# Two-layer GNN kernel: message biases added by a rank-one product on TensorE, evicted by ScalarE, and 72 constant fills moved to the head of GpSimd's queue

## The chip, the cores and the metric

The kernel runs on one core of one Trainium2 chip. The metric is the device time of one execution in microseconds (us). A profile is one further execution, taken by the hardware profiler; it has a time of its own.

## The reference

There are 12,500 nodes with 128 features and 412,500 directed edges sorted by destination. Only the first layer matters here:

```python
h = relu(layernorm(x))
Xs = h[src]
m_data = Xs @ W_data.T + b_data
m_ctrl = Xs @ W_control.T + b_control
msg = where(edge_types == 0, m_data, m_ctrl)
agg = segment_sum(msg, dst)
x = x + relu(agg + (h @ W_self.T + b_self))
```

The second layer gates each message with a tanh of two projections and sums it again by destination.

## The kernel before

**The stages.** The trace shows a front of some 357 us, then loop 0 (layer 0's aggregation, to about 3,390 us), the change to layer 1, and loop 1 (layer 1's aggregation, to the end). The change lies wholly in the front and in what loop 0 does first.

**The front** interleaves two pieces of work, both written as Python generators: `nodes()`, with 14 batches of 7 blocks of 128 nodes, and the search (`edges`, `windows`, `places`/`sought`). For each batch of `nodes()` the program takes four steps of the search; before the fourteenth batch the search is run out. A list scheduler at compile time orders each engine's queue; nothing is reordered at run time, and an engine waits at the head of its queue.

For one block `nodes()` does this: ScalarE makes `h` (L381, layer norm and ReLU); TensorE transposes it into PSUM (`pt`, L384); ScalarE copies that to `hT` (L386); TensorE multiplies by the three weight matrices side by side (`py`, 128 x 384, fp32, L388, two records a product in the profile); VectorE adds the biases while it moves `py` from PSUM to `y` (L390). For one batch VectorE also takes the statistics (L218, L219), GpSimd fills the 129th column of `y` with ones and zeros (L378, L379), SP writes the message rows to the DRAM table `table1` (L391), ScalarE's queue issues the write of the self term (L395), and ScalarE and GpSimd split `h` into three bf16 parts (L398 to L402). `pt`, `py`, `hT`, `h`, `xb` and `y` have two buffers each.

```python
y = pool.tile([P, NBATCH, 3, D + 1], F32, name="y")
nc.gpsimd.memset(y[:, :, 0:2, D:], 1.0)
nc.gpsimd.memset(y[:, :, 2, D:], 0.0)
...
py = ps_y.tile([P, 3, D], F32, name="py")
nc.tensor.matmul(py.rearrange("p k d -> p (k d)"), hT,
                 wT.rearrange("p k d -> p (k d)"), start=True, stop=True)
nc.vector.tensor_add(y[:, i, :, :D], py, bias)
```

The search first reads and transposes the edge lists (`edges`: `raw_...` loads on SP's queue, VectorE arithmetic, transposes at L513, copies `col` at L515), then finds the windows of each chunk of edges (L416 to L445), then locates edges by GpSimd's indirect DMAs: 21 steps of counting (`junk`, L540), 21 `line` gathers (L550), and 7 triples of `g` gathers (L588), each followed by a chain of VectorE operations from L600 to L637, transposes (L581) and copies (L582, L641). `g` has one buffer, so a triple starts when the chain before it has let go.

**Loop 0** works on 469 groups of four tiles of 128 edges. For a group GpSimd issues four indirect gathers from `table1` (`M`, L690; eight buffers of four gathers), VectorE makes a one-hot matrix (`oh`, L701) and TensorE sums (`acc`). Between two groups TensorE works on a dense part for the last 42 node blocks: `oq` and `oc` on VectorE (L794, L796), the product `pa`, its eviction `A` on ScalarE (L799), and the product `z` of `A` with `H`. TensorE products are kept in program order; all of them show as L259, the line of a helper.

Between the groups the program also takes one step at a time of `prepared_for()`. Its first step fills DRAM with zeros (14 large transfers on SP's queue, L726). Its second step makes two flags, one for each loop. For each flag GpSimd fills a row `early` piece by piece with constants known when the program is built (8 and 64 fills, L747), and VectorE compares it with the window starts (L748). `early` has one buffer, so the fills for the second flag wait until the first flag's use of it is over (L754).

```python
early = pool.tile([1, n], F32, name="early")
for c in range(n):
    if c == 0 or done[c] != done[c - 1]:
        nc.gpsimd.memset(early[:, c:], float(done[c]))
nc.vector.tensor_tensor(early, BASE[0:1, :n], early, op=ALU.is_lt)
```

`brow` is a row of the two message biases, each followed by a one, that the dense part of loop 0 uses as one row of a product (the rows `misc<-brow,n` of the profile).

Of the kernel before, what the change touches and what calls it, by code (L numbers as in the profile page):

```python
# [9 lines left out]
F32 = mybir.dt.float32  # L10
# [4 lines left out]
ALU = mybir.AluOpType  # L15
# [3 lines left out]
P = 128  # L19
D = 128  # L20
# [16 lines left out]
def kernel(  # L37
# [32 lines left out]
    nc = tc.nc  # L70
# [93 lines left out]
    ones = consts.tile([P, P], F32, name="ones")  # L164
# [4 lines left out]
    BASE = consts.tile([P, NCK], F32, name="BASE")  # L169
# [165 lines left out]
    with ExitStack() as first:  # L335
# [6 lines left out]
        nc.gpsimd.iota(half[:, P:], pattern=[[1, NCOL]], base=1, channel_multiplier=0,  # L342
                       allow_small_or_imprecise_dtypes=True)
        wz = layer0.tile([P, 2, D + 1], F32, name="wz")
        brow = layer0.tile([1, 2, D + 1], F32, name="brow")
        nc.gpsimd.memset(H[:, :, 3 * D:], 1.0)
        nc.gpsimd.memset(wz[:, :, D:], 0.0)
        nc.gpsimd.memset(brow, 1.0)
        nc.vector.tensor_copy(brow[:, :, :D], bias[0:1, 0:2, :])

        pool = first.enter_context(tc.tile_pool(name="loop0", bufs=1))
        OK = pool.tile([P, 2], F32, name="OK")
# [5 lines left out]
        def nodes():  # L358
            with tc.tile_pool(name="nodes", bufs=2) as pool, \
                    tc.tile_pool(name="nodes_t", bufs=2, space=PSUM) as ps_t, \  # L360
                    tc.tile_pool(name="nodes_y", bufs=2, space=PSUM) as ps_y:
                wT = pool.tile([P, 3, D], F32, name="wT", bufs=1)
                shared["tmin"] = pool.tile([P, TD], F32, name="tmin", bufs=1)
                for k, w in enumerate((w_data, w_control, w_self)):
                    wk = pool.tile([P, D], F32, name="wk", bufs=1)
                    nc.scalar.dma_start(wk, w)
                    pt = ps_t.tile([P, D], F32, name="pt")
                    nc.tensor.transpose(pt, wk, ident)
                    nc.scalar.copy(wT[:, k, :], pt)
                nc.vector.tensor_copy(wz[:, :, :D], wT[:, 0:2, :])  # L370

                for b0 in range(0, NB, NBATCH):
                    xb = pool.tile([P, NBATCH, D], F32, name="xb")
                    load_nodes(xb, b0)
                    rs, shift = scales(pool, xb)
                    h = pool.tile([P, NBATCH, D], F32, name="h")
                    y = pool.tile([P, NBATCH, 3, D + 1], F32, name="y")
                    nc.gpsimd.memset(y[:, :, 0:2, D:], 1.0)  # L378
                    nc.gpsimd.memset(y[:, :, 2, D:], 0.0)  # L379
                    for i in range(NBATCH):  # L380
                        nc.scalar.activation(h[:, i, :], xb[:, i, :], AF.Relu,  # L381
                                             bias=shift[:, i:i + 1], scale=rs[:, i:i + 1])
                        pt = ps_t.tile([P, P], F32, name="pt")
                        nc.tensor.transpose(pt, h[:, i, :], ident)  # L384
                        hT = pool.tile([P, P], F32, name="hT")
                        nc.scalar.copy(hT, pt)  # L386
                        py = ps_y.tile([P, 3, D], F32, name="py")
                        nc.tensor.matmul(py.rearrange("p k d -> p (k d)"), hT,  # L388
                                         wT.rearrange("p k d -> p (k d)"), start=True, stop=True)
                        nc.vector.tensor_add(y[:, i, :, :D], py, bias)  # L390
                    nc.sync.dma_start(  # L391
                        table1[b0 * P * 2:(b0 + NBATCH) * P * 2, :].rearrange(
                            "(b p t) d -> p b (t d)", p=P, t=2),
                        y[:, :, 0:2, :].rearrange("p b t d -> p b (t d)"))
                    nc.scalar.dma_start(agg1[b0 * P:(b0 + NBATCH) * P, :].rearrange(  # L395
                        "(b p) d -> p b d", p=P), y[:, :, 2, :])
                    part = H[:, b0:b0 + NBATCH, :]
                    nc.scalar.copy(part[:, :, :D], h)  # L398
                    nc.gpsimd.tensor_sub(h, h, part[:, :, :D])
                    nc.scalar.copy(part[:, :, D:2 * D], h)  # L400
                    nc.gpsimd.tensor_sub(h, h, part[:, :, D:2 * D])
                    nc.scalar.copy(part[:, :, 2 * D:3 * D], h)  # L402
                    yield
# [318 lines left out]
        def prepared_for(pool):  # L722
            none = pool.tile([P, D], F32, name="none")
            nc.vector.memset(none, 0.0)
            for b0 in range(0, NB, NBATCH):
                nc.sync.dma_start(agg3[b0 * P:(b0 + NBATCH) * P, :].rearrange(  # L726
                    "(b p) d -> p b d", p=P), none[:, None, :].to_broadcast([P, NBATCH, D]))
            nc.sync.dma_start(agg3[NB * P:, :], none)
            nc.sync.dma_start(agg1[NB * P:, :D], none)
            nc.sync.dma_start(agg1[NB * P:, D:], none[:, :1])  # L730
            yield

            need = pool.tile([P, NCK], F32, name="need")
            bad = pool.tile([P, 2], F32, name="bad")
            nc.vector.tensor_scalar(bad, OK, -1.0, 1.0, op0=ALU.mult, op1=ALU.add)
            for k, n, visits, rng in ((0, NC0, MORE0, RNG0), (1, NC2, MORE1, RNG1)):
                nc.vector.tensor_copy(need[:, :n], more[:, :n])
                nc.vector.tensor_scalar(need[:, n:], more[:, n:], 1.0, bad[:, k:k + 1], op0=ALU.add,
                                        op1=ALU.mult)
                nc.vector.tensor_copy(visits, need[0:1, :])  # L740
                bounds(pool, need, rng)

                done, upper = settling[k]
                early = pool.tile([1, n], F32, name="early")
                for c in range(n):
                    if c == 0 or done[c] != done[c - 1]:
                        nc.gpsimd.memset(early[:, c:], float(done[c]))  # L747
                nc.vector.tensor_tensor(early, BASE[0:1, :n], early, op=ALU.is_lt)  # L748
                late = pool.tile([1, n], F32, name="late")
                nc.vector.tensor_scalar(late, BASE[0:1, :n], float(upper - P), None,  # L750
                                        op0=ALU.is_gt)
                nc.vector.tensor_add(early, early, late)
                flag = pool.tile([1, 2], F32, name="flag")
                nc.vector.tensor_reduce(flag[:, 0:1], early, AX.X, ALU.max)  # L754
                nc.vector.tensor_reduce(flag[:, 1:2], need[0:1, :], AX.X, ALU.max)
                nc.vector.tensor_reduce(flag[:, 0:1], flag, AX.X, ALU.max)
                nc.vector.tensor_scalar(flag[:, 0:1], flag[:, 0:1], 0.5, None, op0=ALU.is_gt)
                nc.vector.tensor_copy(AGAIN[:, k:k + 1], flag[:, 0:1])
            yield

            keys = flat_d[T1 - TF:T1 - TF + TDX, :].rearrange("(p t) e -> p (t e)", p=NP)
            at_q = src_q.rearrange("(p t) e -> p (t e)", p=NP)
            at_b = src_b.rearrange("(p t) e -> p (t e)", p=NP)
            W = TDX * P // NP // 13
            for w in range(13):
                ws = slice(w * W, (w + 1) * W)
                shape = [NP, W // 16, 16]
                both = pool.tile([NP, W // 16, 3, 16], F32, name="both")
                nc.sync.dma_start(both.rearrange("p a k e -> p (a k e)"),
                                  keys[:, 3 * w * W:3 * (w + 1) * W])  # L770
                key = both[:, :, 1, :]
                col = pool.tile(shape, F32, name="part")
                nc.vector.tensor_scalar(col, key, 1.0 / P, None, op0=ALU.mult)
                col = floored(pool, col, shape, "part")
                q1 = pool.tile(shape, F16, name="q1", bufs=2)
                nc.vector.scalar_tensor_tensor(q1, col, -float(P), key, op0=ALU.mult, op1=ALU.add)
                nc.sync.dma_start(at_q[:, ws], q1.rearrange("p a e -> p (a e)"))
                up = pool.tile(shape, F32, name="part_up")
                nc.vector.tensor_scalar(up, col, float(NB), None, op0=ALU.is_ge)
                b1 = pool.tile(shape, F16, name="b1", bufs=2)  # L780
                nc.vector.scalar_tensor_tensor(b1, up, -float(NB), col, op0=ALU.mult, op1=ALU.add)
                nc.sync.dma_start(at_b[:, ws], b1.rearrange("p a e -> p (a e)"))
                yield
# [624 lines left out]
```

## Time and profile before

| | us |
|---|---|
| median of 4 runs (lowest, highest) | 7045.01 (7003.73, 7071.27) |
| time of the profiled execution | 7036.41 |
| span of its trace, first to last instruction | 7034.6 |
| PE / DVE / ACT / POOL busy over the span | 5611.8 / 4834.7 / 3176.1 / 3946.5 |
| DVE bias adds of the front (L390, 98) | 53.8 |
| PE message products of the front (L388, 98 in 196 records) | 107.0 |
| last `g` gather of the search, start | 340.95 |
| first `acc` product of loop 0, start | 357.57 |

PE is TensorE, PEld its weight loads, DVE VectorE, ACT ScalarE, POOL GpSimd, SP the engine that only issues DMAs. A row of a timeline gives start, duration, engine, line, operation and, in brackets, the idle time just before and what ended it. "issue" is time for which the profile shows no wait, "remote" a wait whose end it cannot put down to an instruction. PEclk is the TensorE clock that was granted, as a share of full speed; it is read by stage, since a product takes as long as the clock in its stage allows.

### The profile page before, as it was taken

How to read it: one execution, taken by the hardware profiler on the slowest of the kernel's cores; microseconds unless marked ns; L12 is line 12 of the kernel's file. 1: busy time of each engine (PE TensorE's matmuls, PEld its weight loads, DVE VectorE, ACT ScalarE, POOL GpSimd, SP SyncE). 2: the span in 40 equal slices, each digit the busy share in tenths (PEclk: the TensorE clock that was granted, in tenths of full speed). 3: DMA queues.
4: the chain of work that ended last, by engine and by line, in shares of the span. 5: the costliest groups of instructions: out<-in, count | busy, mean ns of one | idle time of the engine just before them, and what ended most of it. 6: DMA issues, size and time to landing. Idle time of an engine off the chain costs nothing. (4 is left out here: it accounts for less than half of the span.)

```text
span 7034.6 us, 108029 instructions
## 1 busy us (share of the span) xinstructions
PE 5611.8 (80%) x33125; PEld 4401.1 (63%) x33126; DVE 4834.7 (69%) x16324; ACT 3176.1 (45%) x9121; POOL 3946.5 (56%) x4224
## 2 busy tenths in 40 slices
PE   5458888888888888888488885888888888888886
PEld 2236666666666666666333332787877877788776
DVE  7656666666576666666477775777777777777775
ACT  5334444444444444444222222655555555555553
POOL 2456656655565656656255655555555555555554
PEclk7669999999999999999799997989999988998898
DMA  6432222222221222221455553122222222222221
GB/s 173 137 91 48 55 49 51 57 57 56 48 69 47 66 49 59 60 56 48 112 145 141 146 139 92 46 53 52 52 54 54 53 54 53 52 53 54 51 52 50
DMA packets 488695, 497.97 MB, mean 71 GB/s; under 512 B 156109, under 2 KB 385897, under 8 KB 488109
## 3 DMA queue, kind: packets, MB, share of 16 engines
q0 software_dynamic: 131360, 274.09, 16.1%
q1 hardware_dynamic: 328141, 201.08, 10.1%
q10 hardware_dynamic: 28608, 15.78, 0.9%
q8 instruction: 271, 4.44, 0.3%
q14 instruction: 315, 2.58, 0.1%
HBM read 415.88 MB, written 74.70 MB: 70 GB/s over the span
## 5 line engine op out<-in xcount | busy, mean ns | idle before, releaser
L974 POOL DMA_INDIRECT M<-table,ix x2128 | 2020.4, 949 | 1563.9 <-issue 806.8
L690 POOL DMA_INDIRECT M<-table,ix x1876 | 1795.4, 957 | 1212.1 <-issue 464.2
L799 ACT CAST A<-pa 128x392 bf16<-128x392 f32 x2688 | 1279.1, 486 | 1506.2 <-PE pa L259 679.6
L259 PE MATMUL z<-H,A 128*128 128x385 bf16 x8232 | 1927.4, 336 | 24.1 <-PE pa L259 15.1
L259 PEld LDWEIGHTS <-A 128*128 128x128 bf16 x8232 | 1134.3, 139 | 893.8 <-issue 607.7
L794 DVE TENSOR_SCALAR oq<-piota,QI 128x128 bf16<-128x128 f16 x2688 | 747.9, 278 | 921.4 <-PE z L259 432.2
L259 PE MATMUL acc<-M,oh 128*128 128x128 f32 (+1 forms) x8008 | 1190.4, 295 | 155.1 <-DVE oh L995 72.2
L259 PEld LDWEIGHTS acc<-M,oh 128*128 128x128 f32 x8008 | 1105.9, 206 | 316.8 <-issue 128.1
L259 PE MATMUL pa<-oc,oq 128*128 128x392 bf16 x2688 | 905.0, 337 | 421.3 <-issue 237.0
L796 DVE TENSOR_SCALAR oc<-piota,CI 128x392 bf16<-128x392 f16 x2688 | 1108.5, 412 | 0.0
L259 PE MATMUL z<-A,HS 128*128 128x128 f32 x6664 | 1010.7, 292 | 93.5 <-issue 77.8
L259 PE MATMUL pa<-oc,oe 128*128 128x196 f32 x4352 | 920.6, 354 | 181.1 <-issue 69.1
L259 PEld LDWEIGHTS z<-A,HS 128*128 128x128 f32 x6664 | 942.9, 205 | 111.3 <-issue 86.4
L259 PEld LDWEIGHTS pa<-oc,oe 128*128 128x128 f32 x4352 | 773.0, 205 | 232.6 <-issue 87.9
L1169 ACT COPY A<-pa 128x392 f32<-128x392 f32 x1088 | 498.0, 484 | 924.5 <-PE pa L259 411.0
L987 ACT ACTIVATE gate<-e,M 128x1 f32<-128x1 f32 x2128 | 516.8, 292 | 650.0 <-DVE only L980 253.2
L980 DVE SCALAR_TENSOR_TENSOR only<-piota,dl,pd 128x128 f32<-128x128 f32 x2128 | 736.9, 346 | 49.5 <-remote 19.6
L1159 ACT ACTIVATE oe<-oq,eb 128x128 f32<-128x128 f32 x2176 | 685.1, 393 | 102.0 <-DVE oq L1151 50.3
L995 DVE TENSOR_SCALAR oh<-piota,dl,e 128x128 f32<-128x128 f32 x2128 | 725.4, 403 | 0.1
L1154 DVE TENSOR_TENSOR oc<-piota,cb 128x784 f32<-128x784 f32 x544 | 525.0, 965 | 29.3 <-remote 11.9
L1151 DVE TENSOR_TENSOR oq<-piota,qb 128x512 f32<-128x512 f32 x544 | 370.6, 681 | 41.9 <-ACT oe L1159 41.9
L259 PE MATMUL ev<-ms,which 98*8 98x512 f32 x552 | 302.9, 632 | 90.6 <-DVE ms L1073 79.4
(271 smaller groups left out, 3390.8 us busy)
## 6 DMA issues: line engine op xcount, KB each, us to landing
M<-table,ix POOLq DMA_INDIRECT x4004
qs<-src_q SPq DMA_DIRECT2D x138, 256.0 KB
bs<-src_b SPq DMA_DIRECT2D x138, 256.0 KB
table<-y SPq DMA_DIRECT2D x14, 903.0 KB
xb<-in_x_dram SPq DMA_DIRECT2D x26, 448.0 KB
o<-agg SPq DMA_DIRECT2D x100, 64.0 KB
agg<-y ACTq DMA_DIRECT2D x14, 451.5 KB
ga<-agg SPq DMA_DIRECT2D x14, 451.5 KB
```

The source lines that it names most:

```text
L259: tc.keep_in_program_order(nc.tensor.matmul(*args, **how))
L690: tc.keep_in_program_order(nc.gpsimd.indirect_dma_start(out=M[:, s, :], out_offset=None, in_=table1, in_offset=bass.IndirectOffsetOnAxis(a ...
L794: nc.vector.tensor_scalar(oq, iota_q, QI[:, k:k + 1], None, op0=ALU.is_equal)
L796: nc.vector.tensor_scalar(oc, iota_c, CI[:, k:k + 1], None, op0=ALU.is_equal)
L799: nc.scalar.copy(A[:, i], pa)
L974: tc.keep_in_program_order(nc.gpsimd.indirect_dma_start(out=M[:, s, :], out_offset=None, in_=table2, in_offset=bass.IndirectOffsetOnAxis(a ...
L980: nc.vector.scalar_tensor_tensor(only, iota_1, dl[:, s:s + 1], pd, op0=ALU.is_equal, op1=ALU.mult, accum_out=e[:, s:s + 1])
L987: nc.scalar.activation(gate[:, s:s + 1], e[:, s:s + 1], AF.Tanh, bias=M[:, s, D:])
L995: nc.vector.tensor_scalar(oh[:, s, :], iota_1, dl[:, s:s + 1], e[:, s:s + 1], op0=ALU.is_equal, op1=ALU.mult)
L1154: nc.vector.tensor_tensor(oc, iota_c[:, None, :].to_broadcast([P, 4, NC1]), cb[:, us, None].to_broadcast([P, 4, NC1]), op=ALU.is_equal)
L1159: nc.scalar.activation(oe[:, k, :], oq[:, k, :], AF.Copy, scale=eb[:, 4 * u + k:4 * u + k + 1])
L1169: nc.scalar.copy(A[:, 4 * u + k:4 * u + k + 2, :], pa)
```

## The change

The biases become a second product into the same PSUM tile: a row of ones (one partition, 128 columns) times a row that holds all three biases and the constants of the 129th column. `py` and the weight tile are widened to 129 columns for each of the three parts, with zeros in the weights' last column; `brow` gets a third part. ScalarE then copies `py` to `y` whole, in place of VectorE's add, and GpSimd's two fills for each batch are gone. Separately, the 72 fills of the flags' rows are issued where the front's constants are made, into two tiles of their own (`taken`) that stay allocated, in place of between groups 1 and 2 of loop 0.

```diff
-        brow = layer0.tile([1, 2, D + 1], F32, name="brow")
+        brow = layer0.tile([1, 3, D + 1], F32, name="brow")
-        nc.gpsimd.memset(brow, 1.0)
-        nc.vector.tensor_copy(brow[:, :, :D], bias[0:1, 0:2, :])
+        nc.gpsimd.memset(brow[:, 0:2], 1.0)
+        nc.gpsimd.memset(brow[:, 2], 0.0)
+        nc.vector.tensor_copy(brow[:, :, :D], bias[0:1, :, :])
+        taken = []
+        for k, (done, _) in enumerate(settling):
+            t = layer0.tile([1, len(done)], F32, name="taken%d" % k)
+            for c in range(len(done)):
+                if c == 0 or done[c] != done[c - 1]:
+                    nc.gpsimd.memset(t[:, c:], float(done[c]))
+            taken.append(t)
...
-                wT = pool.tile([P, 3, D], F32, name="wT", bufs=1)
+                wT = pool.tile([P, 3, D + 1], F32, name="wT", bufs=1)
+                nc.gpsimd.memset(wT[:, :, D:], 0.0)
-                    nc.scalar.copy(wT[:, k, :], pt)
-                nc.vector.tensor_copy(wz[:, :, :D], wT[:, 0:2, :])
+                    nc.scalar.copy(wT[:, k, :D], pt)
+                nc.vector.tensor_copy(wz[:, :, :D], wT[:, 0:2, :D])
...
-                    nc.gpsimd.memset(y[:, :, 0:2, D:], 1.0)
-                    nc.gpsimd.memset(y[:, :, 2, D:], 0.0)
...
-                        py = ps_y.tile([P, 3, D], F32, name="py")
+                        py = ps_y.tile([P, 3, D + 1], F32, name="py")
                         nc.tensor.matmul(py.rearrange("p k d -> p (k d)"), hT,
-                                         wT.rearrange("p k d -> p (k d)"), start=True, stop=True)
-                        nc.vector.tensor_add(y[:, i, :, :D], py, bias)
+                                         wT.rearrange("p k d -> p (k d)"), start=True, stop=False)
+                        nc.tensor.matmul(py.rearrange("p k d -> p (k d)"), ones[0:1, :],
+                                         brow.rearrange("p k d -> p (k d)"), start=False,
+                                         stop=True)
+                        nc.scalar.copy(y[:, i], py)
...
-                done, upper = settling[k]
+                upper = settling[k][1]
                 early = pool.tile([1, n], F32, name="early")
-                for c in range(n):
-                    if c == 0 or done[c] != done[c - 1]:
-                        nc.gpsimd.memset(early[:, c:], float(done[c]))
-                nc.vector.tensor_tensor(early, BASE[0:1, :n], early, op=ALU.is_lt)
+                nc.vector.tensor_tensor(early, BASE[0:1, :n], taken[k], op=ALU.is_lt)
```

## The prediction

> **What bounds the kernel now.** I read the granted clock by stage first, then the stretches of the front, the waits of each engine, the costliest groups, and last the timelines of POOL and PE where loop 0 begins.
>
> Busy time in four stretches of the front (edge reading; windows and counting; line gathers; `g` triples). Columns: stretch, length, busy us of PE, PEld, DVE, ACT, POOL, granted TensorE clock, DMA share, GB/s.
>
> ```profile
> 24.00:120.00 96.00, 59.47 (x210) 34.75 (x209) 70.06 (x215) 58.68 (x137) 22.23 (x32) 0.76 0.74 216
> 120.00:180.00 60.00, 28.93 (x94) 15.01 (x93) 59.16 (x122) 27.00 (x62) 11.52 (x13) 0.73 0.32 85
> 180.00:246.00 66.00, 35.54 (x82) 16.95 (x81) 33.49 (x157) 26.63 (x69) 35.73 (x36) 0.76 0.59 168
> 246.00:310.00 64.00, 32.09 (x90) 15.31 (x89) 49.83 (x118) 26.16 (x62) 25.84 (x25) 0.66 0.43 121
> ```
>
> The reader sees that no one engine bounds the front. DVE does from 120 to 180 us (59.2 of 60). In 24 to 120 DVE, DMA, PE and ACT all lie between 61% and 74%. From 180 us on the search is a chain of gathers and VectorE work, and no engine is over 78%. In loop 0 (460 to 3380 us) PE is busy 2504 of 2920 us at a clock of 0.96, so the loop runs at PE's pace, 6.3 us for a group, while POOL's four gathers of 1.25 us need 5.0. A delay of loop 0's start is therefore not won back: it goes through to the end.
>
> Waits that the change touches, in the front and at loop 0's start: total, times, longest.
>
> ```profile
> DVE y L390 <- PE py L388: 21.3, 26, 2.1
> ...
> POOL y L378 <- DMA agg<-y: 39.8, 8, 10.1
> ...
> POOL early L747 <- DVE flag L754: 19.7, 1, 19.7
> ...
> POOL early L747 <- DMA ci_d<-C: 16.8, 1, 16.8
> ```
>
> DVE stands still for 21.3 us because an add is at the head of its queue before its product is there; the search's VectorE work stands behind it. The last two waits hold POOL at the flags' fills. What they hold back shows in POOL's timeline (start, duration):
>
> ```profile
> 340.95 0.95 POOL L588 DMA_INDIRECT g<-flat_d,rows  x1 [0.30 <-issue]
> 358.72 1.36 POOL L747 MEMSET early<- 1x67 f32 x8 [16.83 <-DMA ci_d<-C]
> 379.79 11.82 POOL L747 MEMSET early<- 1x76 f32 x64 [19.71 <-DVE flag L754]
> 391.77 0.95 POOL L690 DMA_INDIRECT M<-table,ix  x1 [0.16 <-issue]
> ...
> 440.56 0.94 POOL L690 DMA_INDIRECT M<-table,ix  x1 [0.30 <-issue]
> 453.07 0.95 POOL L690 DMA_INDIRECT M<-table,ix  x1 [11.57 <-PE pa L259]
> ```
>
> From 341.9 to 391.8 us POOL issues no gather, though six of the eight `M` buffers are empty. Then it issues 40 in a row. PE over the same time:
>
> ```profile
> 395.09 0.77 PE L259 MATMUL acc<-M,oh 128*128 128x129 f32 x2 [14.61 <-DMA M<-table,ix]
> ...
> 439.35 0.48 PE L259 MATMUL pa<-oc,oq 128*128 128x392 bf16 x1 [27.95 <-issue]
> ...
> 447.04 0.49 PE L259 MATMUL pa<-oc,oq 128*128 128x392 bf16 x1 [6.25 <-ACT A L799]
> ```
>
> PE starves 14.6 us for the third group. Then comes something odd: with all data there, PE, DVE and ACT nearly stop (4.7, 28.0 and 6.3 us idle on PE) until POOL's row of gathers is over. The start of layer 1 shows the same: 28 gathers without a pause from 3481 to 3517 us, and after some 14 of them VectorE stands:
>
> ```profile
> 3481.22 0.94 POOL L974 DMA_INDIRECT M<-table,ix  x1 [98.31 <-issue]
> ...
> 3514.22 0.75 DVE L1073 SCALAR_TENSOR_TENSOR ms<-bs,pidx,gp 98x512 f32<-98x512 f16 x1 [10.92 <-issue]
> ```
>
> I call this the freeze: about 13 gathers (16 us) into an unbroken row the other engines stop, until some 5 us after its end. Two cases make it likely, not sure.
>
> **The change part by part.** Rows for the prices (busy us, mean ns):
>
> ```profile
> L388 PE MATMUL py<-wT,hT 128*128 128x384 f32 x196 | 107.0, 664 | 44.8 <-ACT hT L386 22.9 <-DVE y L390 19.5 <-DVE mv L219 1.0
> L390 DVE TENSOR_TENSOR y<-py,bias 128x384 f32<-128x384 f32 x98 | 53.8, 552 | 22.1 <-PE py L388 21.3
> ...
> L799 ACT CAST A<-pa 128x392 bf16<-128x392 f32 x2688 | 1279.1, 486 | 1506.2 <-PE pa L259 679.6
> ...
> L259 PE MATMUL misc<-wz,zT 128*64 128x129 f32 x336 | 57.6, 296 | 0.5 <-ACT n L815 0.5
> L259 PE MATMUL misc<-brow,n 1*64 1x129 f32 x336 | 57.2, 290 | 0.0
> ```
>
> *The flags' fills.* They cost 1.4 + 11.8 = 13.2 us of POOL wherever they stand. At the head of its queue POOL is idle for 29.3 us (from 3.5 to 32.7 us), so they cost nothing there; behind them stands the new fill of `wT`'s last column, ready near 17 us, and `wT` is first used at 25.1. If that cover were gone, up to 13.2 us would be lost once. They are moved past 40 gathers of `M`, and no DMA moves with them. Without them the 24 gathers of groups 2 to 7 can follow the last `g` gather at 342 us. PE's first `z` comes at 378.7 us; group 2 follows at about 381, and two more groups at 6.3 us put group 4 at 393.6 in place of 451.1: 57.5 us at the most. The freeze eats some of it. It now falls into the row of 24 gathers, 342 to 372 us: it would begin near 358 and end near 377, 19 to 21 us in which the building of `A` stands. The ends are 19 (as in layer 1) and the whole 38.9 + 14.6 of today. I take 21, by the number of gathers: 57.5 - 21 = **36 us gained**, between 4 and 57.
>
> *DVE.* 98 adds go (53.8 us), and 21.3 us of waits with them. This counts only where the search's VectorE work sets the pace. By stretch the adds are 16.9, 10.1, 15.2 and 11.6 us, the waits 10.6, 2.2, 3.3 and 6.6. In 120 to 180 all 12.3 count; in 246 to 310 the chain of a triple takes 14 to 17 us with node work around it and 11.0 without (326.95 to 337.99), so I count half of 18.2, 9; in 180 to 246 DVE waits 28.9 us for gathers, so a quarter of 18.5, 5; in 24 to 120 half of 27.5, 14. Sum: 40 us. All of it at most: 75; nothing at least.
>
> *PE.* 98 products of 387 columns are new. A product with one row costs what one with 128 rows costs (290 against 296 ns), so each is as dear as L388's pair, 1.09 us: 107 us, between 79 (0.81 us a pair, as near 126 us at full clock) and 162 (1.65, at half clock). PE's busy time in 24 to 310 is 156 us of 286; 263 still fits, but bunches no longer do: the search's transposes (L513, L416, L581) stand behind twice the products. The three columns more cost under 1%.
>
> [...]
>
> *ACT.* 98 copies of 128x387 from PSUM: by L799's row 486 ns, 47.6 us on 138 us busy of 286; the idle 148 hides them. The new wait is the dear part: the copy waits for the product, now two, at the head of ACT's queue. Behind it stand the next `hT` (PE waits for it), `h`, and the search's copies `srcf`, `col`, `QI`, `CI`, `yw`; for `col` wait SP's writes. DVE's 21.3 us of waits move here, and each can grow by the second product. The loss by PE and ACT together is shown by no row: nothing if idle time takes it; at most the 107 us of products less PE's waits for DVE's adds (19.5). Nearest is what PE's queue makes the search wait today, 22.9 us for `hT`. I take 22.
>
> *The rest* is nothing: 28 small fills and POOL's 39.8 us wait for `y` go (the add itself never waited for that buffer; if ACT's first copy came early, up to 5.0 us a batch would move to it); `brow`'s copy grows by 128 elements of one partition; SP's `table1` write waits for ACT in place of DVE.
>
> Front: 40 - 22 = **18 us gained**. Sum: 7036.4 - 36 - 18 = 6982.4 us for an execution like the profiled one (span 7034.6, with 1.8 us around it). The median of the runs lies 8.6 us above it, so I forecast **6991 us**. What a measurement of this kernel can tell from no change is about 1%, 70 us.
>
> **The rivals.** Each on the scale of the median.
>
> *All relief, no freeze.* For it: DVE is full from 120 to 180 and PE has 130 us idle. Against: two freezes in the trace. 57 us and the adds and waits of the first, second and fourth stretch (58): 7045 - 115 = 6930.
>
> *The freeze only moves.* Gathers run in a row again, 53.5 us of PE idle return, and the front is neutral: 7045 - 4 = 7041. For it: 38.9 us of the 53.5 have no named cause.
>
> *PE bounds the front (the slower side).* If the clock stays at one half, 98 pairs of products at 1.65 us are 323 us, and PE's other work there is 49: 372 in 286, 86 us over. Less 36: 7045 + 50 = 7095. It decides once PE's mean clock in 24 to 310 is under about 0.65; 0.66 in the last stretch speaks for it, 0.76 in the others against.
>
> *Gathers overtake the search.* Before, eight `M` gathers already went ahead of the last two `g` triples (315 to 326 us). If all 24 do, the search ends 24 x 1.25 = 30 us later: 36 - 30 + 18 = 24 gained, 7021. The fills then are gone, and do not do what they should.
>
> **How the numbers follow.** Forecast 0.40 (own range 6965 to 7020), all relief 0.20, freeze moves 0.18, PE bounds 0.14, overtaking 0.08. For 8 in 10 I reach from the first rival, 6930, to below the slow one, 7085. Faster by over 1% is under 6975: the first rival and a quarter of the forecast, 0.30. Slower by over 1% is over 7115: half of the slow case and a little for a loop order that I can't see, 0.08. Between: 0.62.
>
> **What would show it.** Right: no L747 rows after 340 us, `M` gathers in a row on POOL from about 324, group 4's `acc` near 397 us (451 - 54), the chain of `g` triples ending near 336, DVE under 0.9 in 120 to 180, PEclk in the front over 0.8. Wrong: the last `g` gather later than 345 us, ACT waiting for `py` over 60 us, PE over 90% busy in the front, or a group 4 no earlier than 440.

## The result, and the profile after

The changed kernel is a little **slower**: 7072.11 us median (7027.2 to 7106.04, 52 runs) against 7054.87 us (7003.73 to 7103.06, 78 runs), a ratio of 1.0022 with a 95% interval of 1.0011 to 1.0033; the forecast was 6991 us. Its profiled execution took 7082.81 us, with a span of 7081.1.

The front is where the two traces part. Three marks are used from here on, each read from the timelines: the end of the search (the product `misc<-total,ones`), and the first `acc` of groups 4 and 8 of loop 0.

| us from the span's start | before | after | difference |
|---|---|---|---|
| last `g` gather issued | 340.95 | 394.23 | +53.3 |
| the search ends | 353.5 | 411.9 | +58.4 |
| from there to group 4 | 97.6 | 63.6 | -34.0 |
| group 4 | 451.1 | 475.5 | +24.4 |
| group 468, the last of loop 0 (first `acc`) | 3411.8 | 3440.8 | +29.0 |

Busy time in five stretches of the front, after (columns as for the kernel before: stretch, length, busy us of PE, PEld, DVE, ACT, POOL, granted TensorE clock, DMA share, GB/s):

```profile
24.00:120.00 96.00, 88.36 (x214) 39.85 (x212) 46.33 (x145) 52.40 (x130) 17.03 (x21) 0.75 0.59 176
120.00:180.00 60.00, 54.25 (x140) 23.13 (x140) 43.72 (x120) 35.56 (x82) 7.80 (x6) 0.68 0.37 103
180.00:246.00 66.00, 63.96 (x93) 20.69 (x92) 24.13 (x96) 27.71 (x67) 26.22 (x22) 0.50 0.44 122
246.00:310.00 64.00, 62.13 (x95) 20.68 (x94) 28.43 (x101) 27.42 (x67) 22.02 (x18) 0.50 0.39 106
310.00:358.00 48.00, 46.57 (x88) 17.42 (x89) 23.49 (x56) 23.50 (x57) 14.15 (x12) 0.50 0.41 111
```

PE is now the engine that bounds the front: it is busy 97% of the time from 180 to 358 us. VectorE is relieved, as the change meant it (46.33 us in place of 70.06 in the first stretch). But the clock column reads 0.50 from 180 us on, where it was 0.76 and 0.66. The columns are means over a stretch: each of the 346 entries of the trace's record of the clock holds 1 or 0.5, and it stands at 0.5 from 144.9 to 469.1 us, 324.3 us on end; the last one-row product starts at 392.8. So TensorE has been granted half its speed just where it had the most to do.

The groups that write or read `py` between 24 and 394 us (busy us, mean ns, idle time before them and what ended it):

```profile
L398 PE MATMUL py<-brow,ones 1*128 1x387 f32 x196 | 150.3, 865 | 0.0
L396 PE MATMUL py<-wT,hT 128*128 128x387 f32 x196 | 150.0, 866 | 10.8 <-ACT hT L394 8.8 <-ACT y L401 0.7
L401 ACT COPY y<-py 128x387 f32<-128x387 f32 x98 | 47.3, 482 | 138.9 <-PE py L398 138.7 <-DMA yn_d<-col 0.2
```

The new product costs 150.3 us, and the old one, which was 107.0, has risen to 150.0: 866 ns for each half of it in place of 664. ScalarE's copies cost what was forecast, 482 ns, and wait 138.7 us for the product. The waits between 24 and 394 us show who stands behind (total, times, longest):

```profile
ACT y L401 <- PE py L398: 138.7, 84, 3.2
...
POOL h L410 <- ACT y L401: 56.3, 2, 31.6
...
DVE junk L564 <- DMA line<-flat_d,tile_i: 48.8, 19, 6.8
```

At loop 0's start the fills of `early` are gone from POOL's timeline, and the gathers of `M` begin 8.3 us after the last `g` gather (start, duration, what it is, idle time before it):

```profile
394.23 0.95 POOL L599 DMA_INDIRECT g<-flat_d,rows  x1 [0.30 <-issue]
402.55 1.20 POOL L701 DMA_INDIRECT M<-table,ix  x1 [5.50 <-issue]
...
447.30 0.95 POOL L701 DMA_INDIRECT M<-table,ix  x1 [0.30 <-issue]
```

PE over the same time shows the freeze again, now between groups 0 and 1 (the `acc` of 416.00 and of 448.44): products of `A` come singly, most of them 2.1 to 3.5 us apart, until POOL's row ends.

```profile
416.00 2.06 PE L259 MATMUL acc<-M,oh 128*128 128x129 f32 x8 [3.61 <-DMA M<-table,ix]
...
439.76 0.49 PE L259 MATMUL pa<-oc,oq 128*128 128x392 bf16 x1 [3.01 <-issue]
...
448.44 1.93 PE L259 MATMUL acc<-M,oh 128*128 128x129 f32 x8
```

### The profile page after: what moved, and what is told of

Its sections match the earlier page's. It is cut to its first block, busy times and chain, and to the rows that moved or that the text cites. A ratio compares the mean times of both kernels' runs of the same rounds, so it can differ in the third digit from the quotient of the medians.

```text
span 7081.1 us, 108339 instructions
## 1 busy us (share of the span) xinstructions
PE 5803.2 (82%) x33321; PEld 4456.2 (63%) x33322; DVE 4787.6 (68%) x16226; ACT 3216.1 (45%) x9215; POOL 3941.5 (56%) x4198
## 5 line engine op out<-in xcount | busy, mean ns | idle before, releaser
L259 PEld LDWEIGHTS acc<-M,oh 128*128 128x128 f32 x8008 | 1090.6, 203 | 303.9 <-issue 97.1
L259 PEld LDWEIGHTS pa<-oc,oe 128*128 128x128 f32 x4352 | 792.3, 209 | 223.5 <-ACT oe L1167 96.3
```

Of the source, the lines that this page charges most:

```text
L259: tc.keep_in_program_order(nc.tensor.matmul(*args, **how))
```

## The experiments

Chips differ more than these kernels do: the kernel before took 7128 and 7144 us (medians) on the chips of the first eight runs below and 5904 and 5905 us on those of the last eight, whose loops run faster. Every ratio is against the kernel before on the same chip. The marks of the front come from one trace each and are compared across chips. Where the front is the same, the search's end differs by up to 7.4 us (353.5 in before, 360.9 in before_mb3; 337.6 to 343.8 in the four traces of rows128 with eight or three buffers), so smaller differences are not read. `py` means are for half a product with `wT` and half a product for the biases (bf16rows: the whole of the second).

| kernel | ratio, 95% | clock in 180:246, 246:310 | `py` means, ns | search ends | group 4 |
|---|---|---|---|---|---|
| before | 1 | 0.76, 0.66 | 664 | 353.5 | 451.1 |
| after | 1.0022 (1.0011 to 1.0033) | 0.50, 0.50 | 866, 865 | 411.9 | 475.5 |
| fills_only | 0.9936 (0.9914 to 0.9957) | 0.71, 0.67 | 681 | 383.0 | 421.6 |
| bias_only | 1.0056 (1.0035 to 1.0078) | 0.50, 0.50 | 850, 848 | 407.1 | 505.0 |
| rows128 | 0.9914 (0.9889 to 0.994) | 0.83, 0.84 | 604, 566 | 337.6 | 400.3 |
| bf16rows | 0.9907 (0.9876 to 0.9939) | 0.74, 0.78 | 630, 385 | 353.1 | 395.3 |
| no_product | 0.9925 (0.9901 to 0.995) | 0.74, 0.69 | 650 | 360.7 | 399.2 |
| dve_evicts | 1.0052 (1.0034 to 1.0071) | 0.50, 0.50 | 882, 886 | 426.2 | 495.3 |
| sel128 | 0.9912 (0.9895 to 0.9928) | 0.84, 0.87 | 598, 553 | 341.2 | 406.9 |
| fills_mb3 | 0.9945 (0.9924 to 0.9965) | 0.68, 0.66 | 696 | 365.6 | 406.5 |
| rows32 | 1.0036 (1.0023 to 1.005) | 0.50, 0.50 | 833, 833 | 401.5 | 440.2 |
| rows64 | 1.0025 (1.0016 to 1.0035) | 0.50, 0.50 | 823, 822 | 396.8 | 437.3 |
| paired | 0.9997 (0.9988 to 1.0006) | 0.55, 0.53 | 790, 782 | 381.0 | 421.7 |
| rows128_mb3 | 0.9859 (0.9844 to 0.9874) | 0.82, 0.85 | 608, 570 | 341.2 | 380.3 |
| rows128_same_chip | 0.9931 (0.9918 to 0.9945) | 0.82, 0.86 | 600, 568 | 343.8 | 382.5 |
| rows128_mb3_same_chip | 0.986 (0.9845 to 0.9875) | 0.82, 0.87 | 600, 560 | 341.1 | 381.5 |
| before_mb3 | 0.9923 (0.991 to 0.9937) | 0.71, 0.66 | 680 | 360.9 | 416.5 |
| rows96 | one run: 5868.24 us | 0.81, 0.79 | 628, 586 | 343.9 | 383.0 |

The last column holds the freeze in some rows and not in others. In before and bias_only it stands between groups 3 and 4, in after, rows128, sel128 and dve_evicts between groups 0 and 2. In rows32, rows64, rows96, paired and rows128_same_chip, all on the faster chips with eight buffers, it stands behind group 4 (19 to 26 us from there to group 5), so their group 4 looks early.

### The two parts, one at a time

**fills_only**: the kernel before, with the flags' constants written first and nothing else.

```diff
+        taken = []
+        for k, (done, _) in enumerate(settling):
...
-                nc.vector.tensor_tensor(early, BASE[0:1, :n], early, op=ALU.is_lt)
+                nc.vector.tensor_tensor(early, BASE[0:1, :n], taken[k], op=ALU.is_lt)
```

> The kernel before with the 72 fills moved to the head of GpSimd's queue, and nothing else. Theory (the start of loop 0 gains what was forecast, the front is lost to the products): the search ends where it did, within 10 us of 354, the fourth group's sums start 34 us earlier than before, near 417, and the total is some 34 us under before, near 7020. Rival (the fills' gain seen in the changed kernel only comes from its later start): group 4 near 450, total near 7055.

**bias_only**: the changed kernel, with the constants written where they were.

> The changed kernel with the fills back between the groups of loop 0: only the bias product and ScalarE's eviction are new. Theory: the search ends near 412 us as in the changed kernel, 98 us pass from there to group 4 as before (near 510), and the total is 58 us over before, near 7113; granted clock 0.5 from 145 us to the end of the front. Rival (the two parts are not independent): the total is within 20 us of before.

fills_only took 7095.79 us, by the ratio 46 us (31 to 61) under the kernel before, and 32 by the medians; bias_only took 7170.31, 40 us (25 to 56) over it by the ratio and 42 by the medians. bias_only's marks are those expected: the search ends at 407.1, and 97.9 us later comes group 4. So the change is a gain and a loss that nearly cancel. At group 4 they are 451.1 - 421.6 = 29.5 us gained and 505.0 - 451.1 = 53.9 lost: together +24.4, which is what the changed kernel shows.

The gain did not come in the way expected. In fills_only the gathers of `M` are ready before the search ends, and 25 of them go ahead of the last two `g` triples in POOL's queue, in place of eight. POOL, then VectorE where it takes up these two triples:

```profile
341.25 0.94 POOL L698 DMA_INDIRECT M<-table,ix  x1 [0.30 <-issue]
342.50 0.95 POOL L596 DMA_INDIRECT g<-flat_d,rows  x1 [0.30 <-issue]
...
363.02 0.94 POOL L698 DMA_INDIRECT M<-table,ix  x1 [0.30 <-issue]
364.27 0.95 POOL L596 DMA_INDIRECT g<-flat_d,rows  x1 [0.31 <-issue]
```

```profile
348.25 0.56 DVE L608 TENSOR_TENSOR g<-g,V 128x384 f32<-128x384 f32 x1 [11.28 <-DMA g<-flat_d,rows]
...
369.81 0.56 DVE L608 TENSOR_TENSOR g<-g,V 128x384 f32<-128x384 f32 x1 [12.32 <-DMA g<-flat_d,rows]
```

The same two in the kernel before:

```profile
332.62 0.56 DVE L600 TENSOR_TENSOR g<-g,V 128x384 f32<-128x384 f32 x1 [7.44 <-DMA g<-flat_d,rows]
...
344.06 0.56 DVE L600 TENSOR_TENSOR g<-g,V 128x384 f32<-128x384 f32 x1 [2.39 <-DMA g<-flat_d,rows]
```

PE's transposes for these triples, in fills_only:

```profile
353.12 0.50 PE L589 MATMUL misc<-identh,q 128*128 128x128 f16 x3 [15.60 <-DVE ty L634]
...
374.69 0.50 PE L589 MATMUL misc<-identh,q 128*128 128x128 f16 x3 [16.65 <-DVE col_f L235]
```

PE's two idle times are 11.57 and 6.51 us in the kernel before. The search ends at 383.0 in place of 353.5, 29.5 us later. Of these, 11.8 were there at the fifth triple, whose work on VectorE starts at 327.8 in place of 316.0, before any of these gathers could hold it up; the other 17.7 came behind them. After the search, group 4 follows in 38.6 us in place of 97.6, and no stop stands there. So the rival of the overtaking gathers came true in fills_only. The freeze did not move into the search, but for some 4 us of short waits at its end: VectorE worked on the sixth triple from 348.3 to 357.5 us, as long as before, within POOL's row of gathers. The net came out near the forecast all the same, by luck.

### Is it the one row?

**rows128**: the same product, with 128 rows of 1/128 and the biases in all partitions in place of one row of ones. The same sum, the same number of columns; the constants of the 129th column move into the tile `bias`.

```diff
-                        nc.tensor.matmul(py.rearrange("p k d -> p (k d)"), ones[0:1, :],
-                                         brow.rearrange("p k d -> p (k d)"), start=False,
+                        nc.tensor.matmul(py.rearrange("p k d -> p (k d)"), share[:128, :],
+                                         bias[:128].rearrange("p k d -> p (k d)"), start=False,
```

> The changed kernel with the one-row product replaced by one of 128 rows: ones/128 times the biases held on all 128 partitions, the same 387 columns in fp32 and the same number of products. Theory (a one-row product does not count as activity, so the clock stays at half): the granted clock in the front is 0.85 or more, a product's record falls from 866 to some 450 to 550 ns, the search ends between 340 and 360 us, total 7000 to 7025. Rival (the clock is low for another reason, or the front is simply too full of products): clock 0.5 from 145 us on, records near 866 ns, search end near 412, total near 7072.

**bf16rows**: the biases split in three bf16 parts that together hold the fp32 value, each in 32 partitions (the last 32 hold zeros), so that the product has 128 rows and one record in the profile.

```diff
+                        nc.tensor.matmul(py.rearrange("p k d -> p (k d)"), share,
+                                         bpart.rearrange("p k d -> p (k d)"), start=False,
```

> [...] ScalarE still evicts. Theory (TensorE's time for the bias is the loss, not ScalarE's eviction): the search ends between 330 and 355 us and the total is 6995 to 7020. Rival (ScalarE's eviction and its wait are the loss): the search ends later than 390 us, total near 7060.

**sel128**: rows128 with 127 of the rows of the stationary operand zero.

```diff
-        nc.vector.memset(share, 0.0078125)
+        nc.vector.memset(share, 0.0)
+        nc.vector.memset(share[0:1, :], 1.0)
```

> The product that adds the biases gets 128 rows, but 127 of the rows of its stationary operand are zeros: row 0 holds ones, and all rows of the moving operand hold the biases. It separates how many rows the product feeds from how many of them carry something. Theory A (the clock answers to the rows that an instruction feeds, whatever values they hold): as with 1/128 in all rows: clock 0.80 to 0.85 in 180 to 310 us, products near 600 and 570 ns, search ends at 325 to 350 us, time 0.989 to 0.994 of the kernel before. Theory B (only rows that carry a value in both operands count): as with one row: clock 0.50, products near 860 ns, search ends at 400 to 420 us, time 1.000 to 1.006. In between, the clock between 0.55 and 0.75, would say that the work in the array itself counts.

Two stretches of rows128 and one of sel128 (180 to 246, 246 to 310; 246 to 310):

```profile
180.00:246.00 66.00, 44.58 (x123) 24.38 (x123) 22.07 (x109) 33.82 (x87) 29.94 (x26) 0.83 0.63 165
246.00:310.00 64.00, 44.34 (x142) 24.41 (x143) 46.88 (x108) 34.45 (x86) 26.32 (x21) 0.84 0.55 139
```

```profile
246.00:310.00 64.00, 42.31 (x147) 22.88 (x146) 46.86 (x109) 36.24 (x91) 25.51 (x20) 0.87 0.57 140
```

With 128 rows the clock is at 0.83 and 0.84 although PE is *less* busy (68%), the products take 604 and 566 ns, and the search ends at 337.6 us, 16 us before that of the kernel before. rows128 gains 0.6% to 1.1% on the kernel before; against fills_only, on the same chip, the intervals overlap. The same edit with fewer rows stays at 0.50 (rows32 and rows64, below), and zeros in the stationary operand serve as well as values (sel128: 0.84 and 0.87; its moving operand holds the biases in all rows). bf16rows makes the new product one record of 385 ns in place of two of 566 and gains no more than rows128 in total (the intervals overlap). no_product, below, has no second product at all and gains no more either (0.9925, with the clock at 0.74 and 0.69): in these three the length of the product does not show in the time. That bf16rows ends the search at 353.1 and rows128 at 337.6 is the gathers' doing: 20 of `M` go ahead of the last two `g` triples in the one, none in the other, and group 4 comes at 395.3 and 400.3.

**rows32**, **rows64** and **rows96** change only `128` and the share in rows128's edit.

> The product that adds the biases gets 32 rows (each holding 1/32) instead of one. [...]

> The product that adds the biases gets 64 rows (each holding 1/64) instead of one. [...]

> One look at the clock with 96 rows in the product that adds the biases (64 rows left it at 0.50 in 180 to 310 us, 128 rows brought 0.82 to 0.84). [...]

The stretch from 246 to 310 us of rows64, then of rows96:

```profile
246.00:310.00 64.00, 62.60 (x102) 21.73 (x103) 29.71 (x92) 28.35 (x71) 16.70 (x13) 0.50 0.47 114
```

```profile
246.00:310.00 64.00, 46.16 (x139) 24.92 (x138) 46.37 (x111) 36.59 (x91) 24.14 (x19) 0.79 0.55 142
```

32 and 64 rows leave the clock at 0.50 in both stretches; 96 rows bring 0.81 and 0.79. Why the two groups differ is not shown.

**paired**: the one-row products again, two node tiles at a time, so that two full products stand next to each other.

```diff
-                    for i in range(NBATCH):
+                    for i0 in range(0, NBATCH, 2):
...
+                        for n, (i, hT) in enumerate(pys):
...
+                            nc.tensor.matmul(py.rearrange("p k d -> p (k d)"), hT,
...
+                        for i, py in pys:
+                            nc.tensor.matmul(py.rearrange("p k d -> p (k d)"), ones[0:1, :],
...
+                        for i, py in pys:
+                            nc.scalar.copy(y[:, i], py)
```

> As the changed kernel, with one-row products, but two tiles of nodes at a time: first both products with wT, one behind the other, then both one-row products, then both copies. Same instructions in another order. [...] Rival (only the average share of fed rows counts, and the order is nothing): clock 0.50, products near 860 ns, search ends after 400 us, time 1.002 or more.

The order alone brings the search's end from 411.9 to 381.0 and the time to that of the kernel before (0.9997). The clock rises a little, from 0.50 in both stretches to 0.55 and 0.53, so the rival, for which the order is nothing, was wrong. PE in the changed kernel:

```profile
255.47 1.65 PE L398 MATMUL py<-brow,ones 1*128 1x387 f32 x2
257.05 1.66 PE L396 MATMUL py<-wT,hT 128*128 128x387 f32 x2
258.64 1.65 PE L398 MATMUL py<-brow,ones 1*128 1x387 f32 x2
```
There, at half clock, 1.66 us of full product and 1.65 us of one-row product alternate; in paired two full products stand next to each other. Why the clock is higher in that order is not shown.

### What each side is worth without the one-row product

**no_product** leaves the second product out.

```diff
-                                         wT.rearrange("p k d -> p (k d)"), start=True, stop=False)
-                        nc.tensor.matmul(py.rearrange("p k d -> p (k d)"), ones[0:1, :],
-                                         brow.rearrange("p k d -> p (k d)"), start=False,
-                                         stop=True)
+                                         wT.rearrange("p k d -> p (k d)"), start=True, stop=True)
```

> As the changed kernel, without the second product: ScalarE copies the messages out of PSUM and no bias is added (the biases of the messages and the constants of the three added columns are left out). Theory (the one-row product alone cost the front, by its length and by the clock it leaves at half; VectorE's relief and ScalarE's copies are as the prediction had them): the granted clock in 180 to 310 us is back at 0.65 to 0.75, ScalarE waits for `py` under 50 us instead of 138.7, the last product of the messages starts before 300 us instead of 392.8, the search ends at 320 to 345 us, group 4 starts at 385 to 405, and the time is 0.987 to 0.992 of the kernel before (its groups 46 to 66 us earlier than the 451 of before). Rival (ScalarE's eviction at the head of its queue delays hT and the search's copies, product or no product): ScalarE's wait stays over 90 us, the search ends after 375 us, and the time is no better than 0.997.

**dve_evicts** keeps the product and gives the copy back to VectorE.

```diff
-                        nc.scalar.copy(y[:, i], py)
+                        nc.vector.tensor_copy(y[:, i], py)
```

> As the changed kernel, one-row product and all, but VectorE copies the messages out of PSUM as it did before. Theory (TensorE with the one-row products at half clock bounds the front, whichever engine evicts): the clock stays at 0.50 from about 150 us on, both products stay near 860 ns, the search ends at 400 to 425 us as with ScalarE (411.9), VectorE waits for `py` 120 us or more, and the time is 1.000 to 1.008 of the kernel before. Rival (moving the eviction to ScalarE is what cost the time): the search ends at 350 to 385 us, and the time is 0.992 to 0.997.

The copies' group in no_product, then in dve_evicts (24 to 394 us, and 24 to 440):

```profile
L398 ACT COPY y<-py 128x387 f32<-128x387 f32 x98 | 46.4, 481 | 21.0 <-PE py L396 20.2 <-PE pt L521 0.5
```

```profile
L401 DVE COPY y<-py 128x387 f32<-128x387 f32 x98 | 54.8, 559 | 120.2 <-PE py L398 120.1
```

Without the product ScalarE waits 20.2 us for `py` in place of 138.7; with it VectorE waits 120.1. The wait belongs to the product and not to the engine that evicts. no_product's group 4 is at 399.2, 76.3 us before that of the changed kernel (the ratios, 0.9925 and 1.0022, make it some 69 us of the whole time); its search ended later than I expected (360.7, not 320 to 345), since 25 gathers of `M` go ahead of the last two `g` triples, as in fills_only. Against fills_only, which has the same fills and the same 25 gathers ahead, the work on the fifth triple starts 22.0 us earlier, the search ends 383.0 - 360.7 = 22.3 us earlier and group 4 is 22.4 us earlier: that is VectorE's relief, net of ScalarE's new work, as far as one trace each on two chips can tell. dve_evicts ended its search at 426.2, a little past the expected 425.

### The freeze

**fills_mb3** and **before_mb3** are fills_only and the kernel before with three buffers of `M`; **rows128_mb3** is rows128 with three.

```diff
-MB = 8
+MB = 3
```

> The flags' constants are written first of all, the biases are added by VectorE as before, and there are 3 buffers of `M` in place of 8, so that no more than 12 gathers can be issued in a row before TensorE uses the first. Theory (a long unbroken row of gathers on POOL holds up the other engines once it is past some 13 gathers): no stretch of 25 us in which the search or the building of A all but stops; with the constants first and 8 buffers the search ended at 383.0 us, and here it ends at 350 to 360; group 4 starts at 390 to 405 instead of 421.6; the time is 15 to 30 us under that of 8 buffers, 0.989 to 0.992 of the kernel before. Rival (the stop has another cause, such as the gathers' traffic or the search's own chain): the search still ends after 372 us and group 4 after 412, and the time stays at 0.993 or above, more if three buffers starve loop 0.

> The product that adds the biases gets 128 rows (each holding 1/128), and there are 3 buffers of `M` in place of 8. Theory (with 128 rows the search ended at 337.5 us, and the building of A after it was held up to 375 by an unbroken row of gathers; three buffers end such a row at 12): the search ends at 330 to 345 us, group 1 starts within 14 us of group 0 (33 us with 8 buffers), group 4 starts at 370 to 385 instead of 400.3, and the time is 0.986 to 0.992 of the kernel before. Rival (three buffers give back in the loops what they win in front, or the stop has another cause): group 4 at 395 or later, or loop 0 from group 4 to group 468 longer than 3000 us (2991.2 with 8 buffers), and the time at or above that of 8 buffers, 0.9914.

> The 128-row product with 8 buffers of `M` once more, on one chip with the 3-buffer version, because the loops ran 17% faster on the chip of the last four runs. Theory (the three buffers end the stop at loop 0's start and no more): 8 buffers are 15 to 30 us slower than 3 on the same chip, group 4 at 395 to 405 us; the rest of the gain, 45 to 60 us on the kernel before, belongs to the rows and the order of the fills. Rival (the 80 us are the chip's): 8 buffers are within 8 us of 3 buffers.

> The 128-row product with 3 buffers of `M`, the other half of the pair. Theory: group 4 at 370 to 385 us, the time 0.985 to 0.992 of the kernel before and 15 to 30 us under 8 buffers. Rival (on a chip whose loops take 6.4 us a group, three buffers starve them and give the gain back): at or above the time of 8 buffers.

> The kernel before with 3 buffers of `M` in place of 8 and nothing else changed: the flags' constants stay late, VectorE adds the biases. Theory (the near stop of TensorE, VectorE and ScalarE from about 404 to 447 us is the price of the unbroken row of 40 gathers after the fills; three buffers allow 12): PE's building of A goes on without a break after the fills, group 4 starts at 405 to 420 us in place of 451.1, and the time is 0.993 to 0.997 of the kernel before. Rival (the stop comes from the fills or from the data, not from the row): group 4 still starts after 440 us, time 0.998 or more.

PE in before_mb3, from the end of the search on:

```profile
365.02 2.06 PE L259 MATMUL acc<-M,oh 128*128 128x129 f32 x8 [3.57 <-DVE oh L701]
...
402.68 2.38 PE L259 MATMUL acc<-M,oh 128*128 128x129 f32 x6 [16.47 <-DMA M<-table,ix]
...
411.65 1.05 PE L259 MATMUL acc<-M,oh 128*128 128x129 f32 x8
```

The 16.47 us for the third group, behind the late fills, are still there; the stop that followed in the kernel before is not (its trace is from a chip with slower loops; the ratio that follows is from one chip). Group 4 starts at 416.5 in place of 451.1, and the time is 0.9923 (0.991 to 0.9937), better than I had said. On one chip, three buffers took rows128 from 5865.17 to 5823.15 us, 42 us. I was wrong on where: with eight buffers group 4 came at 382.5, as with three (381.5), and the stop stood behind it (PE idle for 18.04 us from 383.5 on), 24.8 us from group 4 to group 5 in place of 9.6. By group 8 eight buffers are 16.9 us behind (424.7 against 407.8), by group 468 44.5 us (2811.1 against 2766.6), so further losses lie inside loop 0. On the chips with the slower loops three buffers won 15.1 us at group 4 (fills_mb3 against fills_only, 406.5 and 421.6) but nothing in the time that these runs can tell (0.9945 and 0.9936): from group 4 to group 468 the traces show 3011.2 us with three and 2993.4 with eight. There all three of my marks were missed; the search ended at 365.6, not 350 to 360. That it ended earlier than in fills_only has a plain reason, no freeze: 12 gathers of `M` go ahead of the last two `g` triples in place of 25.

The trigger stays open. "An unbroken row of some 13 gathers" is not it: in before_mb3 POOL issues 32 gathers in a row at 1.25 us each, from 399.15 to 438.02 us, and PE goes on (5.3 us idle at the most); in rows128_same_chip the row ran 39 gathers, from 334.5 to 382.5 us, before PE stopped. What is shown, on one chip with rows128, is that fewer buffers, which keep POOL from running far ahead of PE, take the stop away (9.6 us from group 4 to group 5 with three, 24.8 with eight).

rows128_mb3 is the fastest version here: 0.9859 (0.9844 to 0.9874) and, on another chip, 0.986 (0.9845 to 0.9875).

## Why the prediction was wrong, step by step

- **Start of loop 0, 36 us gained: right in size, partly by luck.** The traces show 34.0 from the search's end to group 4 (97.6 - 63.6), and fills_only 29.5 net. The freeze taken off, 21, measures 21.1: 32.4 us from group 0 to group 1 after, 11.3 before. But the 21 came from counting gathers in a row, a rule that before_mb3 and rows128_same_chip rule out, and fills_only reached its 29.5 by another way, with gathers ahead of the search and no stop behind it. The range's upper end, 57, also holds no freeze at all; with the smaller of the two sizes given for it, 19 us, it would be 38.5.
- **The fills cost nothing at the head of POOL's queue: right.** The first product with `wT` starts at 25.1 us in both traces.
- **DVE's relief, 40 us, in part.** It can be read only without the one-row product: 22.3 us net of ScalarE's work (no_product against fills_only). With 128 rows the search ends 45.5 us before that of fills_only (383.04 - 337.56), but no `M` gather goes ahead of a `g` gather there and the freeze follows behind; at group 4 rows128 (400.3) and no_product (399.2) are level.
- **ACT's copies, 486 ns: right** (482), as was the place of the new wait. Moving the eviction to ScalarE is not what cost the time: with the product, dve_evicts is no faster than the changed kernel, and no_product gains with ScalarE evicting.
- **PE and ACT together, 22 us lost: the step that failed.** The front was to gain 40 - 22 = 18 us and its search ended 58.4 later. The one-row product costs 76 us at group 4 (475.5 - 399.2). I priced the pair at 1.09 us, 107 us in all, at the clock of the kernel before, and took the old products' price as given. The pair took 1.53 us, 150.3 in all, and the old products rose by 43 us, most of both at half clock. My row for "one row costs what 128 cost" (290 against 296 ns in the loop's tail) is right for the length of an instruction (865 and 866 ns in the changed kernel). It says nothing of the clock, 0.50 with the one-row product and 0.83 and 0.84 with 128 rows (rows128, 180 to 310 us).
- **The clock.** I looked for a clock over 0.8 in the front. That was an estimate: the kernel before shows 0.73 from 24 to 310 us, and the changed kernel 0.62. A busier TensorE did not have the higher clock: 97% busy at 0.50 with one row (180 to 358 us), 68% busy at 0.83 with 128 rows (rows128, 180 to 246 us), and 12% busy at 0.50 in the kernel before (310 to 358 us). What lowers the clock beside one-row products is not shown.
- **The rival that came true** was "PE bounds the front at half clock", at 0.14. Its condition, a mean clock under 0.65, and its signs (PE over 90% busy, ACT waiting over 60 us for `py`, the last `g` gather after 345) are all in the trace (0.62 from 24 to 310 us, 94%, 138.7 us, 394.2). It said +86 and -36; the search ended 58.4 us later and 34.0 came back. It overshot: it held the whole front at half clock, and from 24 to 180 us the clock was at 0.75 and 0.68.
- **The delay goes through to the end: right in kind.** Group 4 is 24.4 us later, group 468 29.0, and the medians differ by 17.2.

## What to carry to other kernels

In these kernels a one-row product cost twice: by its own length (865 ns a half) and by the clock, which read 0.50 where it had read 0.76 and 0.66, so that the products beside it took 866 ns in place of 664. So a bias added by a row of ones belonged on all 128 partitions (a share in each, 0.9914, or zeros in all but one row of the stationary operand, 0.9912), or next to others of its kind and not between full products (0.9997, against 1.0022). When work moves to TensorE, read the granted clock by stage in the profile after, before the busy time: PE at 97% with the clock at 0.50 was not an engine at its limit. When work moves off an engine's queue, ask what then goes ahead of what: with the fills gone, gathers of `M` overtook the search. And a prefetch depth is a cost as well as a cover: three buffers of gathers beat eight in two kernels here (42 and 47 us), both on the chips with the faster loops; with the slower loops fills_mb3 gained nothing (0.9945, against 0.9936 with eight).

## What was not expected of the hardware

- TensorE stayed at half clock for 324.3 us while it was 97% busy from 180 to 358 us, with one-row products between full ones. From 180 to 310 us the clock read 0.50 with 32 and 64 rows too, 0.79 to 0.87 with 96 and 128 in fp32, and 0.74 and 0.78 with 128 in bf16 (bf16rows); with 127 of 128 rows of the stationary operand zero it read 0.84 and 0.87.
- While POOL issued gathers far ahead of PE, PE, VectorE and ScalarE nearly stopped, with data there: 21 us in the changed kernel, and three buffers in place of eight were worth 42 us in rows128 and 47 us in the kernel before, on one chip. What starts the stop is open.
- The same kernel took 7.1 ms on some chips and 5.9 ms on others; with rows128, loop 0's groups took 6.4 us (2991.2 us from group 4 to group 468) on one and 5.2 us (2428.6) on another. From 560 to 2760 us, within loop 0, PE is busy 85% of the time on the slower one (rows128, 1867.9 of 2200 us, clock 0.96) and over 98% on faster ones (rows64, 2169.7 of 2200 us; rows128_mb3, 2186.9; clock 1.00 in both); on the slower it stands 173.8 us before `pa` products for nothing that the profile shows. Why is open.
